# A deformable-convolution and attention kernel: batch 0's samples transposed by TensorE into two buffer sets, and three head groups that run chunks 4 and 5 apart

## The chip, the cores and the metric

The kernel runs on one core of one Trainium2 chip. The metric is the device time of one execution in microseconds; lower is better. Engines: TensorE (PE, with its weight load PEld), VectorE (DVE), ScalarE (ACT), GpSimd (POOL) and SyncE (SP, which here only issues DMAs).

## The reference

The input x is (4, 128, 64, 64) in float32: four batches, 128 channels, 64 x 64 positions. Cut to what matters:

```python
# layer 0: deformable 3x3 convolution on the group-normalized input
offset, mask = conv2d(gn(x), w_off), sigmoid(conv2d(gn(x), w_mask))   # 18 + 9 per position
samples = bilinear_sample(gn(x), position + tap + offset) * mask      # b, c, 9 taps, h, w
x = x + einsum("bckhw,ock->bohw", samples, w) + bias
# layer 1: tokens t = (b, 4096, 128)
z = layer_norm(t)
q = qz_ring(z.heads(16, 8) + rx)          # cosines and their products along the 8
attn = softmax(q @ q.T / sqrt(8)) @ q     # 16 heads, 4096 x 4096 scores each
x1 = layer_norm(z + attn @ w_comb.T + b_comb)
t = t + layer_norm(x1 + relu(zf(x1) @ w1.T + b1) @ w2.T + b2)
t = t + top2_of_8_experts(layer_norm(t))
```

Queries, keys and values are the same q, so the scores are symmetric: the exponentials of key chunk i against query chunk j, transposed, serve key chunk j against query chunk i.

## The kernel before

**Units of work.** A batch's 4096 positions are eight chunks of 512 (`NCH`, `CH`); the 16 heads are four groups of four (`NGRP`). One attention *step* is 128 keys of one group against one chunk of 512 queries: `scores` (L1261, TensorE into two PSUM tiles of tag `sc`, of which there are three), two exponentials of 128 x 1024 (L1270, ScalarE), `context` (L1281, TensorE, into the one accumulator `acc`; the row of ones in the values gives the softmax's denominator). A *run* is the steps of one group and one query chunk; `runs` lists them in order. `WHOLE` runs take all 32 steps at once. Batch 0's chunks become ready one after the other, so its first 26 runs (`opening`) and some after them take only the key chunks that are there: `FIRST` starts a sum, `MORE` and `LAST` go on with it; between them the sum lies in DRAM (`partd`, stored at L1126, loaded into `cu` at L1456). In the opening ScalarE takes the sum out of `acc` (L1491), and a sum loaded into `cu` is added by a product with the identity (L281 on `acc`); after it VectorE does both (L1493, L1495). `gifts` names the pairs of chunks where the exponentials are turned by VectorE (`turn`, L1140), stored (`etd`), fetched again (`fetch`, L1195) and used by a later run (`from_turned`, L1214) in place of its own steps.

**Making a chunk.** `prepare(b)` norms the batch, writes a table of corner values to DRAM, makes offsets and weights, and then `deform` goes through 96 units (chunk, three taps, 128 positions). A unit is three indirect DMAs of GpSimd (L625; `gather` keeps some units ahead), a weighting and two sums on VectorE (L645, L650, L651). The sampled values lie with positions on partitions, and the convolution needs channels there. For chunks 0 and 1 of batch 0 TensorE transposes a unit into the one PSUM bank `misc` (L662) and VectorE copies it into `sT_first` (L665). For all others VectorE transposes 32 x 32 blocks (L686) and the chunk goes out to `smd` in DRAM (L698) and comes back in the other order (L731, `sT`). `convolved` then does the convolution (`conv_ps`), adds x (`xr`, L758), and `features` makes q and its high and low parts (`hiT`, `loT`, L838, L839), copies the values into `fx` on GpSimd (L823), and stores the operands (`fqd` L827, `kTd` L846, `qTd` L847). `finish` does the work after the attention (projection, feed-forward, experts) for a chunk of which all four groups are done; up to two of them are under way.

**The order.** PE, DVE, SP and POOL run in the order in which the program issues (`tc.manual_schedule`). A planner, `Beside`, decides that order: it keeps a clock `now` that moves on `STEP` = 1.82 us a step, a due time of VectorE (`dve`), and a queue of generators (`prepare`, `finish`, `turned`) that yield what they want next (`need(pe, dve, lat, hold, after)`). At each step it lets in side work: TensorE pieces (`fills`, one a step or three, within `credit`) and VectorE pieces as long as VectorE is at most `backlog` behind. `hold=True` keeps the `misc` bank for one job, `hold=None` stands outside that lock. `later` issues a DMA or a GpSimd instruction at a due time. When no step can go on for want of a chunk, `force` lets side work in without a step.

The lines below are those that no other place of this text says.

```python
STEP = 1.82; RATE = 0.44; LATE = 0.50
NV = 3; NF2 = 11; NST = 3; NET = 2; NCU = 2
ps_s = ctx.enter_context(tc.tile_pool(name="ps_s", bufs=3, space=PSUM))
```

Of the kernel before, what the change touches and what calls it, by code (L numbers as in the profile page):

```python
# [22 lines left out]
P = 128  # L23
# [7 lines left out]
KK = 9  # L31
# [193 lines left out]
def kernel(  # L225
# [373 lines left out]
    def deform(b, tab, idx, wt, rest):  # L599
# [8 lines left out]
        def early(n):  # L608

            return b == 0 and n < 3 * 12  # L610
# [23 lines left out]
        for n, (ch, kg, j) in enumerate(units):  # L634
# [11 lines left out]
            if moved:  # L646
                yield need(pe=0.01, dve=ve(384))
                moved.pop()()
# [3 lines left out]
            if b == 0 and ch < 2:  # L652


                if n % 12 == 0:
                    while len(summed) < ch:
                        yield need(lat=0.5)
                    sT = big.tile([P, KK, CH], F32, tag="xs", name=f"sT_first{ch}")
                yield need(pe=tr(3), lat=FREE, hold=True)
                pt = misc(f"sT_ps{j}_{kg}")  # L660
# [3 lines left out]
                def move(sT=sT, kg=kg, i=j % 4, pt=pt):  # L664
                    nc.vector.tensor_copy(  # L665
                        sT[:, 3 * kg : 3 * kg + 3, P * i : P * (i + 1)],
                        pt[:, : 3 * P].rearrange("p (k c) -> p k c", c=P),
                    )
# [3 lines left out]
                if n % 12 == 11:  # L672
                    yield need(pe=0.01, dve=ve(384))
# [45 lines left out]
    def convolved(b, ch, sT=None):  # L719
# [4 lines left out]
        if not in_order:  # L724
            yield need(lat=2.5)

            sT = big.tile([P, KK, CH], F32, tag="xs", name=f"sT{b}_{ch}")

        def get(kg):
            for c in range(4):  # L730
                nc.sync.dma_start(  # L731
                    out=sT[32 * c : 32 * (c + 1), 3 * kg : 3 * kg + 3],
# [8 lines left out]
        for k in range(KK):  # L741
            if k == 2 and not in_order:
                get(2)
            for hf in range(2):
                last = k == KK - 1 and hf == 1
                yield need(pe=MM256, dve=ve(128, 4) if last else 0.0, lat=0.2 if last else FREE, hold=not last)
                if k == 0 and hf == 0:
# [3 lines left out]
                    sT[:, k, 256 * hf : 256 * (hf + 1)], k == 0 and hf == 0, last,  # L751
# [41 lines left out]
    def features(b, ch, x2, mean, rstd):  # L793
# [29 lines left out]
        beside.later(beside.dve, lambda: nc.gpsimd.tensor_copy(f4[:, :, :, :HD], q8))  # L823

        def put_values():
            for g in range(NGRP):
                nc.sync.dma_start(out=fqd[b % 2][ch][g], in_=fx[:, :, QG * g : QG * g + QL])  # L827

        beside.later(beside.dve + 2.0, put_values)
# [3 lines left out]
        yield need(pe=tr(4), dve=ve(512, 2))  # L833
# [5 lines left out]
        nc.vector.tensor_tensor(lo.bitcast(F32R), pt, hi, ALU.subtract)  # L839

        def put(part, fT):

            kd = kTd[b % 2][ch].rearrange("(h l r d) n -> l r h d n", l=2, r=2, d=HD)
            qd = qTd[b % 2][ch].rearrange("(h r l d) n -> l r h d n", l=2, r=2, d=HD)
            for rep in range(2):
                nc.sync.dma_start(out=kd[part, rep], in_=fT)  # L846
                nc.sync.dma_start(out=qd[part, rep], in_=fT)  # L847

        beside.later(beside.dve - ve(512), lambda: put(0, hi))
        beside.later(beside.dve, lambda: put(1, lo))  # L850
# [69 lines left out]
    def feed_forward(b, ch, x4, a4):  # L920

        z3 = [
# [42 lines left out]
        nc.vector.tensor_tensor(a4, a4, pf.rearrange("p (i c) -> p i c", c=C), ALU.add)  # L965
        m = work.tile([P, 4], F32, tag="ln_m", name=f"m2{b}_{ch}")
# [156 lines left out]
    def park_sums(g, sc, cu, when):  # L1123
# [6 lines left out]
        beside.later(when, put)  # L1130
# [96 lines left out]
    groups, done, active = {}, [], []  # L1227
# [67 lines left out]
    def gifts(b, g, sc):  # L1295
        first = (4 if g == NGRP - 1 else 3) if b == 0 else 0
        return [sc + 1] if first <= sc < NCH - 1 else []
# [35 lines left out]
    for sc in range(4):  # L1333
        add_run(0, NGRP - 1, sc, [4, 5], MORE)
    for g in (3, 0, 1, 2):
        for sc in range(4):
            add_run(0, g, sc, range(6 if g == 3 else 4, 8), LAST)
# [72 lines left out]
    with tc.manual_schedule(engines={PE, DVE, SP, POOL}):  # L1410
# [6 lines left out]
        while n < len(steps):  # L1417
# [20 lines left out]
            beside.fills = 3 if run < 12 else 1  # L1438
            if streaming:
                backlog = 1.5  # L1440
# [49 lines left out]
            if by_act:  # L1490
                nc.scalar.copy(cu, acc)  # L1491
            elif kind in (WHOLE, FIRST):
# [5 lines left out]
            else:  # L1498
                park_sums(g, sc, cu, beside.now + 3.0 if by_act else beside.dve)
# [75 lines left out]
```

## Time and profile before

| | |
|---|---|
| median of the runs | 7609.23 us (7607.39 to 7621.65, 3 runs) |
| profiled execution | 7579.71 us |
| its span, first to last instruction | 7576.5 us, 180754 instructions |
| busy: PE, DVE, ACT, POOL | 94%, 59%, 91%, 22% |
| mean granted TensorE clock | 0.968 |
| exponentials (L1270) | 7400, 6849.4 us busy |
| turned pieces (L1140) | 792 transposes, 396 stores and 396 fetches |

The profile shows one execution. Busy time of an engine is counted without its register, branch, semaphore and DMA-issuing instructions. A wait is put down to the event that came last before the engine went on. L12 is line 12 of the kernel; a line can be that of a helper, as L281 for every product in four column groups.

### The profile page before, as it was taken

The numbers are of one execution on the slowest core, as the hardware profiler recorded it, in microseconds if no ns is written. First come the engines' busy times: TensorE is split into PE (matmuls) and PEld (weight loads), VectorE is DVE, ScalarE is ACT, GpSimd is POOL, SyncE is SP. The second block draws the span as 40 slices with busy tenths as digits, with TensorE's granted clock in tenths as the row PEclk, the third lists the DMA queues.
The fourth block names the chain that finished last, engine by engine and source line by source line (L and its number), as shares of the span: only waits on it lengthen the run. The fifth ranks groups of instructions, "written<-read, shape, count | busy, mean of one in ns | idle before, by whom it ended". The sixth has DMA issues, their size and how long they took to land.

```text
span 7576.5 us, 180754 instructions
## 1 busy us (share of the span) xinstructions
PE 7113.9 (94%) x73848; PEld 2375.9 (31%) x73848; DVE 4465.9 (59%) x8950; ACT 6863.5 (91%) x7467; POOL 1653.2 (22%) x1326
## 2 busy tenths in 40 slices
PE   3688999899999999999999999999999999999997
PEld 2122222223333333333333323333333333333333
DVE  7755356667444877776544677775444554455434
ACT  0578999889999999999999998989999999999995
POOL 5544034443000433422000334431000000000000
PEclk6889999999999999999999999999999999999998
DMA  6777567978446878887655789897454466666661
GB/s 181 223 204 219 141 223 241 300 234 291 149 168 200 292 244 280 268 277 244 203 179 190 228 279 298 289 324 237 174 190 152 148 236 230 232 222 239 226 202 63
DMA packets 909788, 1689.51 MB, mean 223 GB/s; under 512 B 150754, under 2 KB 384124, under 8 KB 858268
## 3 DMA queue, kind: packets, MB, share of 16 engines
q1 hardware_dynamic: 809102, 1371.37, 54.9%
q0 software_dynamic: 92160, 302.06, 12.4%
q8 instruction: 579, 9.49, 0.5%
q10 hardware_dynamic: 7694, 4.52, 0.2%
q14 instruction: 253, 2.07, 0.1%
HBM read 1027.51 MB, written 650.14 MB: 221 GB/s over the span
## 4 chain that ended last, share of the span: by engine, by line
PE 80%; DMA 8%; DVE 4%; issue 2%; ACT 2%; SPq 1%; another core or an unknown queue 0%; POOL 0%; POOLq 0%; DVEq 0%; ACTq 0%
PE acc L1281 39%; PE sc L1261 24%; PE acc L1214 5%; PE e_ps L281 4%; PE conv_ps L281 3%; DMA et<-etd 2%; PE f_ps L281 2%; ACT e L1270 2%; DMA etd<-st 1%; DMA sT<-smd 1%; PE om_ps L533 1%; DMA smd<-tr 1%; DVE st L1140 1%; DVE v L645 1%; DMA cu<-part 1%
## 5 line engine op out<-in xcount | busy, mean ns | idle before, releaser
L1270 ACT ACTIVATE e<-sc 128x1024 f32<-128x1024 f32 x7400 | 6849.4, 1081 | 527.0 <-PE sc L1261 368.1
L1281 PE MATMUL acc<-e,qf 128*9 128x512 f32 (+1 forms) x29600 | 3938.3, 601 | 18.6 <-ACT cu L1491 7.5
L1261 PE MATMUL sc<-qT,kT 32*128 32x512 f32 x14800 | 2368.7, 499 | 153.3 <-ACT e L1270 84.8
L1261 PEld LDWEIGHTS sc<-qT,kT 32*128 32x128 f32 x14800 | 942.8, 183 | 3612.6 <-ACT e L1270 3130.4
L625 POOL DMA_INDIRECT v<-tab,idx x1152 | 1451.8, 1260 | 1579.3 <-DVE tr L686 956.2
L1140 DVE STREAM_TRANSPOSE st<-e 128x1024 f32<-128x1024 f32 x792 | 937.3, 1222 | 752.4 <-ACT e L1270 620.1
L1281 PEld LDWEIGHTS acc<-e,qf 128*9 128x9 f32 (+1 forms) x29600 | 682.4, 91 | 610.3 <-issue 346.8
L396 POOL TENSOR_TENSOR r<-ln_t,expo 128x4 f32<-128x4 f32 x96 | 112.2, 1169 | 3105.4 <-DVE ln_t L394 3057.0
L645 DVE TENSOR_TENSOR v<-v,wt 128x1536 f32<-128x1536 f32 x384 | 667.0, 1737 | 119.5 <-DMA v<-tab,idx 96.8
L1214 PE MATMUL acc<-et,qv 128*9 128x128 f32 x12672 | 506.4, 276 | 52.2 <-DMA et<-etd 44.6
L1065 DVE TENSOR_TENSOR eo<-e_ps,gt 128x512 f32<-128x512 f32 x256 | 175.2, 686 | 552.5 <-PE e_ps L281 547.5
L650 DVE TENSOR_TENSOR v<-v 128x768 f32<-128x768 f32 x384 | 367.2, 956 | 10.1
L281 PE MATMUL conv_ps<-sT,wconv_sb 128*32 128x256 f32 x4320 | 351.0, 399 | 15.7 <-DMA sT<-smd 11.6
L1214 PEld LDWEIGHTS acc<-et,qv 128*9 128x9 f32 x12672 | 270.0, 90 | 254.4 <-issue 212.6
L686 DVE STREAM_TRANSPOSE tr<-v 128x128 f32<-128x128 f32 x1080 | 249.4, 282 | 37.5 <-DMA etd<-st 28.7
L1493 DVE COPY cu<-acc 128x512 f32<-128x512 f32 x116 | 80.2, 692 | 306.3 <-PE acc L1281 260.8
L651 DVE TENSOR_TENSOR v<-v 128x384 f32<-128x384 f32 x384 | 215.7, 562 | 13.3
L396 POOL TENSOR_TENSOR rstd<-lt_t,expo 128x4 f32<-128x4 f32 x32 | 57.9, 1811 | 575.9 <-DVE lt_t L394 550.7
L281 PE MATMUL f_ps<-w_sb,h 128*32 128x128 f32 x4096 | 166.1, 282 | 0.1
L950 DVE TENSOR_SCALAR h<-h_ps,b_sb 128x512 f32<-128x512 f32 x128 | 94.9, 744 | 100.3 <-PE h_ps L948 89.9
L823 POOL COPY fx<-rn 128x512 f32<-128x512 f32 x32 | 26.8, 838 | 526.3 <-DVE rn L822 321.4
L965 DVE TENSOR_TENSOR a<-a,f_ps 128x512 f32<-128x512 f32 x32 | 21.9, 685 | 198.8 <-PE f_ps L281 198.8
(227 smaller groups left out, 3166.9 us busy)
## 6 DMA issues: line engine op xcount, KB each, us to landing
etd<-st SPq DMA_DIRECT2D x396, 1024.0 KB
et<-etd SPq DMA_DIRECT2D x396, 1024.0 KB
kT<-kTd SPq DMA_DIRECT2D x372, 256.0 KB
smd<-tr SPq DMA_DIRECT2D x360, 192.0 KB
sT<-smd SPq DMA_DIRECT2D x360, 192.0 KB
qT<-qTd SPq DMA_DIRECT2D x166, 256.0 KB
atd<-cu SPq DMA_DIRECT2D x128, 256.0 KB
qf<-fqd SPq DMA_DIRECT2D x372, 72.0 KB
```

What stands on the lines that cost most here:

```text
L281: nc.tensor.matmul(dst[c : c + 32], lhsT=lhsT[:, c : c + 32], rhs=rhs, start=start, stop=stop)
L625: nc.gpsimd.indirect_dma_start(out=v[:, k, :], out_offset=None, in_=tab, in_offset=bass.IndirectOffsetOnAxis(ap=idx[:, j, kk : kk + 1], ax ...
L645: nc.vector.tensor_tensor(v4, v4, w12[:, :, None].to_broadcast([P, 12, C]), ALU.mult)
L650: nc.vector.tensor_tensor(v[:, :, : 2 * C], v[:, :, : 2 * C], v[:, :, 2 * C :], ALU.add)
L651: nc.vector.tensor_tensor(v[:, :, :C], v[:, :, :C], v[:, :, C : 2 * C], ALU.add)
L686: nc.vector.transpose(out=tr9[:, k, :, j % 4, :], in_=v[:, k, :C].rearrange("p (c i) -> p c i", i=32),)
L1065: nc.vector.tensor_tensor(ws[hf], pe.rearrange("p (e c) -> p e c", c=C), gt[:, i, 4 * hf : 4 * (hf + 1), None].to_broadcast([P, 4, C]), AL ...
L1140: nc.vector.transpose(out=st[:, :, 2 * pr : 2 * pr + 2, :].rearrange("p o h (q j) -> p o (h q) j", j=32), in_=es[pr].rearrange("p h (q o i ...
L1214: nc.tensor.matmul(acc[32 * h : 32 * h + QW, P * kt : P * (kt + 1)], lhsT=qv[:, at : at + QW], rhs=e[:, :, h, 32 * t : 32 * (t + 1)], star ...
L1261: nc.tensor.matmul(ps[i // 2][:, i % 2, :], lhsT=kT[h : h + 32, P * (t % 4) : P * (t % 4 + 1)], rhs=qT[h : h + 32, :], start=True, stop=True,)
L1270: nc.scalar.activation(e, ps[pr], AF.Exp, scale=1.0 / math.sqrt(HD))
L1281: nc.tensor.matmul(acc[32 * h : 32 * h + width, :], lhsT=flat[:, first : first + width], rhs=es[h // 2][:, h % 2, :], start=(t == ts[0]), ...
```

## The change

- For all chunks of batch 0 the samples are transposed by TensorE, into a PSUM tile of tag `sc` and outside the lock of `misc`; the copy out is three copies of 128 columns. The target alternates between the tile `xs` (even chunks) and nine tiles of tag `f2` (odd chunks), and the next chunk's units wait for the convolution of the chunk before the last, not of the last. Gathers run four units ahead for the whole batch.
- In the opening the planner lets three TensorE pieces in per step for all 26 runs (before: 12), and VectorE may be 4.0 us behind (before: 1.5).
- For all batches: the copy into `fx` is VectorE's, after `loT`; operands are stored with one DMA for the values (before: four) and two for each of the high and low parts (before: four), with another order of the rows inside a head, the same for keys and queries.
- `feed_forward` waits while another one is under way (`heavy`).
- A partial sum of the opening is stored from ScalarE's queue straight after its copy.
- Groups 3, 2 and 1 take chunks 4 and 5 for query chunks 0 to 2 in runs of their own (before: group 3, query chunks 0 to 3), and the order of the groups is 3, 2, 1, 0 (before: 3, 0, 1, 2). `gifts` starts at chunk 3 for all groups of batch 0.

```diff
--- before.py
+++ after.py
@@ -607,7 +607,7 @@
 
         def early(n):
 
-            return b == 0 and n < 3 * 12
+            return b == 0
 
         def gather(last):
 
@@ -644,33 +644,41 @@
             yield need(dve=ve(1536), after=landed)
             nc.vector.tensor_tensor(v4, v4, w12[:, :, None].to_broadcast([P, 12, C]), ALU.mult)
             if moved:
-                yield need(pe=0.01, dve=ve(384))
+                yield need(dve=ve(128, 3))
                 moved.pop()()
             yield need(dve=ve(768) + ve(384))
             nc.vector.tensor_tensor(v[:, :, : 2 * C], v[:, :, : 2 * C], v[:, :, 2 * C :], ALU.add)
             nc.vector.tensor_tensor(v[:, :, :C], v[:, :, :C], v[:, :, C : 2 * C], ALU.add)
-            if b == 0 and ch < 2:
+            if b == 0:
 
 
                 if n % 12 == 0:
-                    while len(summed) < ch:
+                    while len(summed) < ch - 1:
                         yield need(lat=0.5)
-                    sT = big.tile([P, KK, CH], F32, tag="xs", name=f"sT_first{ch}")
-                yield need(pe=tr(3), lat=FREE, hold=True)
-                pt = misc(f"sT_ps{j}_{kg}")
+                    if ch % 2:
+                        sT = [
+                            work.tile([P, CH], F32, tag="f2", name=f"sT{ch}_{k}", bufs=NF2)
+                            for k in range(KK)
+                        ]
+                    else:
+                        sT = big.tile([P, KK, CH], F32, tag="xs", name=f"sT_first{ch}")
+                        sT = [sT[:, k] for k in range(KK)]
+                yield need(pe=tr(3), lat=FREE, hold=None)
+                pt = ps_s.tile([P, 2, 512], F32, tag="sc", name=f"sT_ps{j}_{kg}")[:, 0, :]
                 for k in range(3):
                     nc.tensor.transpose(pt[:, P * k : P * (k + 1)], v[:, k, :C], ident)
 
                 def move(sT=sT, kg=kg, i=j % 4, pt=pt):
-                    nc.vector.tensor_copy(
-                        sT[:, 3 * kg : 3 * kg + 3, P * i : P * (i + 1)],
-                        pt[:, : 3 * P].rearrange("p (k c) -> p k c", c=P),
-                    )
+                    for k in range(3):
+                        nc.vector.tensor_copy(
+                            sT[3 * kg + k][:, P * i : P * (i + 1)], pt[:, P * k : P * (k + 1)]
+                        )
 
                 moved.append(move)
                 beside.later(beside.now + 0.8, lambda n=n: gather(n))
                 if n % 12 == 11:
-                    yield need(pe=0.01, dve=ve(384))
+                    yield need(lat=0.6)
+                    yield need(dve=ve(128, 3))
                     moved.pop()()
                     featuring.append(True)
                     beside.add("prepare", convolved(b, ch, sT), 0.5, True)
@@ -724,12 +732,13 @@
         if not in_order:
             yield need(lat=2.5)
 
-            sT = big.tile([P, KK, CH], F32, tag="xs", name=f"sT{b}_{ch}")
+            sTs = big.tile([P, KK, CH], F32, tag="xs", name=f"sT{b}_{ch}")
+            sT = [sTs[:, k] for k in range(KK)]
 
         def get(kg):
             for c in range(4):
                 nc.sync.dma_start(
-                    out=sT[32 * c : 32 * (c + 1), 3 * kg : 3 * kg + 3],
+                    out=sTs[32 * c : 32 * (c + 1), 3 * kg : 3 * kg + 3],
                     in_=smd[ch % 2][:, 3 * kg : 3 * kg + 3, c].rearrange("i k o n -> i k (o n)"),
                 )
 
@@ -748,7 +757,7 @@
                     po = misc(f"conv_ps{b}_{ch}")
                 by_columns(
                     po[:, 256 * hf : 256 * (hf + 1)], wconv_sb[:, k, :],
-                    sT[:, k, 256 * hf : 256 * (hf + 1)], k == 0 and hf == 0, last,
+                    sT[k][:, 256 * hf : 256 * (hf + 1)], k == 0 and hf == 0, last,
                 )
         summed.append(True)
         for o in range(4):
@@ -820,34 +829,35 @@
         nc.vector.tensor_tensor(q8[:, :, :, 1], c8[:, :, :, 0], c8[:, :, :, 1], ALU.mult)
         for d in range(2, HD):
             nc.vector.tensor_tensor(q8[:, :, :, d], q8[:, :, :, d - 1], c8[:, :, :, d], ALU.mult)
-        beside.later(beside.dve, lambda: nc.gpsimd.tensor_copy(f4[:, :, :, :HD], q8))
-
-        def put_values():
-            for g in range(NGRP):
-                nc.sync.dma_start(out=fqd[b % 2][ch][g], in_=fx[:, :, QG * g : QG * g + QL])
-
-        beside.later(beside.dve + 2.0, put_values)
-
-
-
-        yield need(pe=tr(4), dve=ve(512, 2))
+
+
+
+        yield need(pe=tr(4), dve=ve(512, 3))
         pt = misc(f"fT_ps{b}_{ch}")
         for i in range(4):
             nc.tensor.transpose(pt[:, P * i : P * (i + 1)], n[:, P * i : P * (i + 1)], ident)
         hi, lo = temp("hiT"), temp("loT")
         nc.vector.tensor_copy(hi.bitcast(F32R), pt)
         nc.vector.tensor_tensor(lo.bitcast(F32R), pt, hi, ALU.subtract)
+        nc.vector.tensor_copy(f4[:, :, :, :HD], q8)
 
         def put(part, fT):
 
-            kd = kTd[b % 2][ch].rearrange("(h l r d) n -> l r h d n", l=2, r=2, d=HD)
-            qd = qTd[b % 2][ch].rearrange("(h r l d) n -> l r h d n", l=2, r=2, d=HD)
-            for rep in range(2):
-                nc.sync.dma_start(out=kd[part, rep], in_=fT)
-                nc.sync.dma_start(out=qd[part, rep], in_=fT)
-
-        beside.later(beside.dve - ve(512), lambda: put(0, hi))
-        beside.later(beside.dve, lambda: put(1, lo))
+            kd = kTd[b % 2][ch].rearrange("(p l r) n -> l p r n", l=2, r=2)
+            qd = qTd[b % 2][ch].rearrange("(p r l) n -> l p r n", l=2, r=2)
+            twice = fT[:, None, :].to_broadcast([P, 2, CH])
+            nc.sync.dma_start(out=kd[part], in_=twice)
+            nc.sync.dma_start(out=qd[part], in_=twice)
+
+        def put_values():
+            nc.sync.dma_start(
+                out=fqd[b % 2][ch].rearrange("g p t x -> p t g x"),
+                in_=fx.rearrange("p t (g x) -> p t g x", g=NGRP),
+            )
+
+        beside.later(beside.dve - 2.0 * ve(512), lambda: put(0, hi))
+        beside.later(beside.dve - ve(512), lambda: put(1, lo))
+        beside.later(beside.dve, put_values)
         prepared[b, ch] = beside.dve + 9.0
         featuring.pop(0)
 
@@ -919,6 +929,9 @@
 
     def feed_forward(b, ch, x4, a4):
 
+        while heavy:
+            yield need(lat=1.0)
+        heavy.append(True)
         z3 = [
             work.tile([P, 4, HD], F32, tag=f"zf{k}", name=f"zf{k}{b}_{ch}") for k in range(3)
         ]
@@ -963,6 +976,7 @@
                     f == 0, f == FFN // P - 1,
                 )
         nc.vector.tensor_tensor(a4, a4, pf.rearrange("p (i c) -> p i c", c=C), ALU.add)
+        heavy.pop()
         m = work.tile([P, 4], F32, tag="ln_m", name=f"m2{b}_{ch}")
         rs = work.tile([P, 4], F32, tag="ln_r", name=f"r2{b}_{ch}")
         yield from layer_norm_stats(a4, m, rs, "ln")
@@ -1120,14 +1134,14 @@
 
         beside.later(beside.dve, put)
 
-    def park_sums(g, sc, cu, when):
+    def park_sums(g, sc, cu):
 
         def put():
             nc.sync.dma_start(out=partd[g][sc], in_=cu)
             storing.discard((g, sc))
 
         storing.add((g, sc))
-        beside.later(when, put)
+        beside.later(beside.dve, put)
 
 
 
@@ -1224,7 +1238,7 @@
 
     landing = {}
     fetched = {}
-    groups, done, active = {}, [], []
+    groups, done, active, heavy = {}, [], [], []
 
     def finishing():
 
@@ -1293,8 +1307,7 @@
     gives, takes = set(), {}
 
     def gifts(b, g, sc):
-        first = (4 if g == NGRP - 1 else 3) if b == 0 else 0
-        return [sc + 1] if first <= sc < NCH - 1 else []
+        return [sc + 1] if (3 if b == 0 else 0) <= sc < NCH - 1 else []
 
 
     def add_run(b, g, sc, chunks, kind):
@@ -1330,11 +1343,12 @@
     opening = len(runs)
     for g in range(2, NGRP):
         extend(g, range(2), [2, 3], MORE)
-    for sc in range(4):
-        add_run(0, NGRP - 1, sc, [4, 5], MORE)
-    for g in (3, 0, 1, 2):
+    for g in (3, 2, 1):
+        for sc in range(3):
+            add_run(0, g, sc, [4, 5], MORE)
+    for g in (3, 2, 1, 0):
         for sc in range(4):
-            add_run(0, g, sc, range(6 if g == 3 else 4, 8), LAST)
+            add_run(0, g, sc, range(6 if g and sc < 3 else 4, 8), LAST)
         for sc in range(4, 8):
             add_run(0, g, sc, range(NCH), WHOLE)
 
@@ -1435,9 +1449,9 @@
                     gives.remove(steps[m])
                     turn(es[m - n], *steps[m])
 
-            beside.fills = 3 if run < 12 else 1
+            beside.fills = 3 if streaming else 1
             if streaming:
-                backlog = 1.5
+                backlog = 4.0
             else:
                 backlog = 0.4 if at >= len(ts) - 3 else 3.2
             if b + 1 < NB:
@@ -1489,14 +1503,15 @@
                 cu = work.tile([P, 512], F32, tag="cu", name=f"cu{run}", bufs=NCU)
             if by_act:
                 nc.scalar.copy(cu, acc)
+                nc.scalar.dma_start(out=partd[g][sc], in_=cu)
             elif kind in (WHOLE, FIRST):
                 nc.vector.tensor_copy(cu, acc)
             else:
                 nc.vector.tensor_tensor(cu, cu, acc, ALU.add)
             if kind in (WHOLE, LAST):
                 park_context(b, g, sc, cu)
-            else:
-                park_sums(g, sc, cu, beside.now + 3.0 if by_act else beside.dve)
+            elif not by_act:
+                park_sums(g, sc, cu)
         alone.append(True)
         beside.drain()
```

## The prediction

> **What bounds the kernel now.** I read the page first, then busy time by stage, then the waits and the chain of the first 900 us. From the page:
>
> ```profile
> PE 7113.9 (94%) x73848; PEld 2375.9 (31%) x73848; DVE 4465.9 (59%) x8950; ACT 6863.5 (91%) x7467; POOL 1653.2 (22%) x1326
> ACT  0578999889999999999999998989999999999995
> L1270 ACT ACTIVATE e<-sc 128x1024 f32<-128x1024 f32 x7400 | 6849.4, 1081 | 527.0 <-PE sc L1261 368.1
> ```
>
> One attention step (`steps[n]`, 128 keys against 512 queries of four heads) has two of these exponentials. 6849.4 us over 7400 is 0.926 us each (neighbours overlap, so less than the mean of one), 1.85 us a step for 3700 steps. ScalarE is the floor; the time can only move where ScalarE is idle, or by taking steps away. Its idle time is mostly early, so next the stages (columns: us, busy time and count of PE, PEld, DVE, ACT, POOL, then TensorE clock, DMA share, GB/s):
>
> ```profile
> 0.00:182.00 182.00, 61.42 (x559) 39.31 (x559) 127.42 (x211) 7.61 (x9) 98.32 (x84) 0.68 0.62 180
> 182.00:320.00 138.00, 78.37 (x685) 25.98 (x685) 102.16 (x188) 59.13 (x67) 84.67 (x63) 0.75 0.73 221
> 320.00:650.00 330.00, 277.14 (x2164) 76.80 (x2160) 200.52 (x365) 260.40 (x289) 160.67 (x123) 0.89 0.75 223
> 650.00:912.00 262.00, 246.21 (x1904) 69.66 (x1900) 130.96 (x266) 241.23 (x262) 60.96 (x47) 0.95 0.52 152
> 912.00:2246.00 1334.00, 1278.74 (x12190) 401.48 (x12186) 776.30 (x1424) 1237.13 (x1342) 387.89 (x311) 0.98 0.72 230
> 2246.00:5900.00 3654.00, 3548.07 (x38068) 1192.36 (x38068) 2311.73 (x4601) 3467.55 (x3764) 819.87 (x659) 0.99 0.72 238
> ```
>
> ScalarE idles 78.9 + 69.6 + 20.8 = 169 us between its first exponential (182) and 912, where batch 0's chunks are still being made; 97 us to 2246; 186 us to 5900. What it waits for in the first 900 us:
>
> ```profile
> ACT e L1270 <- PE sc L1261: 212.9, 41, 122.4
> PE sc L1261 <- DMA kT<-kTd: 46.9, 4, 22.0
> PEld acc L281 <- DMA cu<-part: 28.5, 5, 8.2
> ```
>
> Scores wait for keys of a chunk that is not yet there, context sums for a parked partial sum. The chain shows why the latter is late (start us, length):
>
> ```profile
> 261.38 5.98 DMA qf<-fqd
> 268.64 1.38 SPq L698
> 271.08 6.51 DMA sT<-smd
> 277.61 6.89 DMA cu<-part
> 284.54 1.93 PE acc L281 x8
> ```
>
> On SP's queue the partial sum stands behind the samples' trip through DRAM (L698 out, L731 back). By the timeline, batch 0's chunks have their operands issued to DRAM at 162, 254, 356, 471, 580, 692, 793 and 875: 82 to 115 us apart. The attention has done 16 steps at 221, 64 at 390, 104 at 477, 160 at 641, 256 at 826; it cannot pass 16, 64, 104 and 256 steps without chunks 1, 2, 3 and 4/5. It waits for chunk 1 (45.6 us at 222) and chunk 3 (14.0 at 478). The other 110 us are small: partial sums 28.5, `conv_ps` behind samples 9.4, the key load behind batch 1's border DMAs at 890 10.8, the rest in gaps under 5 us.
>
> **The change, part by part.** *Samples by TensorE, two buffer sets.* One unit (three taps of 128 positions) on VectorE now:
>
> ```profile
> 207.83 1.75 DVE L645 TENSOR_TENSOR v<-v,wt 128x1536 f32<-128x1536 f32 x1
> 209.62 0.96 DVE L650 TENSOR_TENSOR v<-v 128x768 f32<-128x768 f32 x1
> 210.61 0.56 DVE L651 TENSOR_TENSOR v<-v 128x384 f32<-128x384 f32 x1
> 211.20 0.70 DVE L686 STREAM_TRANSPOSE tr<-v 128x128 f32<-128x128 f32 x3
> ```
>
> That is 4.0 us. In chunks 2 to 7 (72 units) the last row gives way to three 128x128 copies out of PSUM. The trace has 128x384 at 0.551 and 128x512 at 0.69, so 0.27 each and 0.82 a unit: 4.1 us. Features take 19 us of VectorE per chunk (the sum of L758 to L839 in the timeline) and 0.6 more for the copy into `fx` (GpSimd's median 0.612; no VectorE row of this shape, a 128x512 tensor_tensor takes 0.69). A chunk is 12 x 4.1 + 19.6 = 69 us of VectorE and 36 x (1.31 + 0.30) = 58 us of gathers, against 105 us between chunks now. What held it there goes: the DRAM trip, two units gathered ahead instead of four, `len(summed) < ch`, and the 1.5 us that VectorE might be behind in the opening. At 75 us a chunk, chunk 2 is there near 330, chunk 3 near 405 and chunk 7 near 700, each before the attention asks. The GpSimd copy, for which gathers stood in line (98.5 us idle before seven of them), is gone as well.
>
> TensorE gets 216 transposes; three of them start 0.109 us apart at 190.7, so 24 us over some 500 us. A step needs about 1.29 us of TensorE (scores 0.43, context 0.86 by start times at 812), so 1.85 - 1.29 a step hides them. [...]
>
> *What is new on TensorE's queue.* The transposes wait in order for the sums of a VectorE that may now be 4 us behind, and all scores and context products queue behind them; and they sit in one of the three `sc` buffers until the copies, one multiply later, some 3 of every 4 us. No row shows this with attention at full rate. The nearest are three units at 182 to 192, where ScalarE had gaps of 3.89, 1.72 and 1.58 us: 2.4 a unit. The other end is 0, if the slack takes it. I take 0.5 (36 us for 72 units): those three stood behind VectorE waiting 2.07 and 0.86 us for gathers, with ScalarE one step ahead; later four units are gathered ahead and TensorE is late itself, so VectorE is mostly done.
>
> *Partial sums stored from ScalarE's queue*, 26 of them, each behind its copy, with the next exponential behind it. From SP the issue takes 0.33 us; with the copy's 0.585 waited out, 0.91. So 9 to 24 us; I take 0.6 each, 16 us. It frees SP, which waited 113.8 us for these copies. [...]
>
> *Three groups with [4, 5] apart.* Chunks 6 and 7 are asked for at step 328 instead of 288, so the 10.8 us at 890 are covered. Nine such runs replace four: five more accumulator hand-overs at 29.3/72 = 0.4 us, +2. One more chunk is turned instead of recomputed: four steps fewer, -7.4.
>
> *Batches 1 to 3.* Twelve operand DMAs a chunk become five, and SP no longer stands before `fqd` for GpSimd:
>
> ```profile
> SPq L827 <- POOL fx L823: 171.7, 26, 14.2
> SPq L1195 <- PE acc L1214: 590.7, 159, 9.5
> ```
>
> Behind it are the turned tiles (L1195), for which TensorE waited 44.6 + 32.9 us. At best half of that, 40, comes back; at worst VectorE's 32 x 0.6 = 20 is added; `heavy` only spaces the feed-forward parts, with nothing late behind it in the trace. I take -12.
>
> **The sum.** ScalarE's idle time from 182 to 912: 169 becomes 35 (chunk 1, a little earlier by SP's shorter queue) + 5 (partial sums) + 20 (small gaps) + 16 + 36 = 112, so -57. With -7, +2 and -12: -74. The profiled execution took 7579.7 (span 7576.5 and 3.2 around it), which gives 7506; the median of the runs is 29.5 higher, so 7609 - 74 = 7535.
>
> **The rivals.** *TensorE's order costs the gain (slower).* At 2.4 us for each of 72 units, 173 instead of 36: 63 us slower, 7672. It decides from 1.5 us a unit. For it: the three gaps at 182. Against: TensorE waiting that long means VectorE is the limit, and 69 us a chunk leave it idle a third of the time at today's rate. *All cover holds.* No cost on the queue (-36), 9 for the stores (-7), 40 back in the later batches (-28): 7464. For it: nothing but ScalarE bounds after 5900, so each gap closed is kept. *Nothing arrives.* The 110 us of small gaps are the planner's, not the chunks', and stay at 75 rather than 25: 7585 to 7610. [...]
>
> **How the numbers follow.** Forecast (7500 to 7585) 0.58, all cover holds 0.17, nothing arrives 0.11, slower 0.14. About 0.2%, 15 us, is what a measurement of this kernel can tell from no change: faster is the first two and a third of the third, 0.79; same 0.07; slower 0.14. The range leaves out the ends of both outer cases: 7455 to 7610.
>
> **What would show it.** Right: 7392 exponentials; operands of chunk 7 stored near 700; 160 steps done near 555 instead of 641; ScalarE idle some 110 us in its first 730; TensorE's clock above 0.9 from 320 on; no `smd` before batch 1. Wrong: `sT_ps` waits on VectorE of over 1.5 us a unit, chunks still 100 us apart, or idle time after 912 that grows by what the opening gave.

## The result and the profile after

The change made the kernel slower: 7680.7 us (median of 4 runs, 7674.25 to 7697.35) against 7608.3 for the kernel before (4 runs beside them), a ratio of 1.0097, 95% interval 1.0075 to 1.0119, 72 us. The profiled execution took 7697.35 (span 7695.5), 17 above the median, where that of before lay 29 below its own; so the two traces stand 118 us apart and show some 45 more than the change is worth.

The page of the kernel after, the same three lines as before:

```profile
PE 7167.8 (93%) x74144; PEld 2403.9 (31%) x74144; DVE 4478.0 (58%) x9043; ACT 6865.9 (89%) x7459; POOL 1600.2 (21%) x1294
ACT  0678998898999988988999988889999999999995
L1284 ACT ACTIVATE e<-sc 128x1024 f32<-128x1024 f32 x7392 | 6851.0, 1076 | 649.6 <-PE sc L1275 464.8
```

The floor held: 7392 exponentials, 6851.0 us, 0.927 us each. What grew is ScalarE's idle time before an exponential, 649.6 us against 527.0, and the eights in its row stand in the middle of the program as well as at its beginning. Busy time by stage of the kernel after (us, busy time and count of PE, PEld, DVE, ACT, POOL, then TensorE clock, DMA share, GB/s):

```profile
182.00:320.00 138.00, 95.46 (x734) 32.77 (x734) 95.92 (x197) 61.87 (x68) 77.68 (x63) 0.78 0.58 182
320.00:650.00 330.00, 287.74 (x2238) 88.84 (x2230) 208.68 (x404) 255.82 (x281) 145.69 (x117) 0.92 0.57 173
650.00:912.00 262.00, 242.67 (x1915) 70.22 (x1917) 120.24 (x237) 239.81 (x258) 56.09 (x48) 0.96 0.43 132
912.00:2246.00 1334.00, 1261.43 (x12190) 398.59 (x12183) 790.44 (x1441) 1225.53 (x1327) 382.83 (x304) 0.98 0.74 239
2246.00:5900.00 3654.00, 3475.83 (x36912) 1163.54 (x36908) 2249.22 (x4455) 3368.01 (x3655) 797.76 (x640) 0.98 0.71 234
```

ScalarE's idle time: 172.5 us from 182 to 912 (169.2 before, 112 forecast), 108.5 to 2246 (96.9 before), and 286.0 from 2246 to 5900, where it was 186.5. So the opening gained nothing, and the loss is almost all in batches 1 and 2, which the change hardly seems to touch. Waits of the kernel after from 182 to 912 (engine, tile, line, what ended the wait; us in total, times, longest):

```profile
ACT e L1284 <- PE sc L1275: 110.0, 82, 33.0
ACT cu L1505 <- PE acc L281: 26.8, 7, 14.8
PE acc L281 <- DMA cu<-part: 10.5, 1, 10.5
PE sT_ps L669 <- DVE v L651: 14.3, 7, 4.3
POOL v L625 <- PE sT_ps L669: 266.5, 30, 32.9
```

The wait for keys (`kT<-kTd`) is gone, as is most of that for partial sums. TensorE's transposes wait 14.3 us in all for VectorE; gathers wait 266.5 us for TensorE's transposes, which free their `v` tiles. In batches 1 and 2, 2246 to 5900 us, the kernel before had

```profile
ACT e L1270 <- PE sc L1261: 96.3, 89, 8.1
PE acc L1214 <- DMA et<-etd: 20.7, 8, 6.7
PE conv_ps L281 <- DMA sT<-smd: 4.1, 2, 3.8
```

and the kernel after

```profile
ACT e L1284 <- PE sc L1275: 169.8, 113, 14.9
PE acc L1228 <- DMA et<-etd: 52.7, 15, 9.6
PE conv_ps L281 <- DMA sT<-smd: 20.8, 4, 13.7
```

TensorE, in order, waits longer and more often for the turned tiles that it uses instead of recomputing exponentials, and for samples that come back from DRAM (chunks of batches 1 to 3 still take that way); ScalarE waits for the scores queued behind them. These two waits grew by 49 us; the rest of the 99 is spread over other waits.

### The profile page after: what moved, and what is told of

Same layout as the page of the kernel before. It is cut to its first block, busy times and chain, and to the rows that moved or that the text cites. A ratio compares the mean times of both kernels' runs of the same rounds, so it can differ in the third digit from the quotient of the medians.

```text
span 7695.5 us, 180911 instructions
## 1 busy us (share of the span) xinstructions
PE 7167.8 (93%) x74144; PEld 2403.9 (31%) x74144; DVE 4478.0 (58%) x9043; ACT 6865.9 (89%) x7459; POOL 1600.2 (21%) x1294
## 4 chain that ended last, share of the span: by engine, by line
PE 81%; DMA 7%; DVE 4%; ACT 3%; issue 3%; SPq 1%; POOL 1%; another core or an unknown queue 1%; ACTq 0%; POOLq 0%; DVEq 0%
PE acc L1295 39%; PE sc L1275 24%; PE acc L1228 5%; PE conv_ps L281 4%; PE e_ps L281 3%; ACT e L1284 3%; DMA et<-etd 2%; PE f_ps L281 2%; DMA sT<-smd 1%; POOL v L625 1%; PE om_ps L533 1%; DVE v L645 1%; SPq L730 1%; PE ao_ps L281 1%
## 5 line engine op out<-in xcount | busy, mean ns | idle before, releaser
L1284 ACT ACTIVATE e<-sc 128x1024 f32<-128x1024 f32 x7392 | 6851.0, 1076 | 649.6 <-PE sc L1275 464.8
L625 POOL DMA_INDIRECT v<-tab,idx x1152 | 1436.1, 1247 | 2212.1 <-DVE tr L694 1340.4
L281 PE MATMUL conv_ps<-sT,wconv_sb 128*32 128x256 f32 x4032 | 328.9, 401 | 47.9 <-DMA sT<-smd 39.8
L694 DVE STREAM_TRANSPOSE tr<-v 128x128 f32<-128x128 f32 x864 | 199.0, 281 | 31.6 <-DMA etd<-st 25.0
L669 PE MATMUL sT_ps<-ident,v 128*128 128x128 f32 x288 | 64.0, 341 | 117.4 <-DVE v L651 76.0
L281 PEld LDWEIGHTS conv_ps<-sT,wconv_sb 128*32 128x32 f32 x4032 | 85.6, 109 | 175.8 <-issue 154.1
```

The source lines that it names most:

```text
L281: nc.tensor.matmul(dst[c : c + 32], lhsT=lhsT[:, c : c + 32], rhs=rhs, start=start, stop=stop)
L625: nc.gpsimd.indirect_dma_start(out=v[:, k, :], out_offset=None, in_=tab, in_offset=bass.IndirectOffsetOnAxis(ap=idx[:, j, kk : kk + 1], ax ...
L694: nc.vector.transpose(out=tr9[:, k, :, j % 4, :], in_=v[:, k, :C].rearrange("p (c i) -> p c i", i=32),)
L1284: nc.scalar.activation(e, ps[pr], AF.Exp, scale=1.0 / math.sqrt(HD))
```

## The experiments

Theories. *Order*: TensorE's queue and the `sc` tile cost what the earlier chunks gain. *Plan*: the opening gains, and other parts of the change (guard, store block, runs) shift side work of the later batches to where TensorE waits. Kernels were measured in sets, each beside runs of the kernel before. Its medians lay between 7461 and 7614 us from set to set, so what is compared across sets is the ratio to its runs in the same set. That a ratio carries over from one set to another was not measured.

**Parts of the change, alone or taken away.** In the change, the guard is on from `feed_forward`'s first line to its sum:

```diff
     def feed_forward(b, ch, x4, a4):
+        while heavy:
+            yield need(lat=1.0)
+        heavy.append(True)
...
         nc.vector.tensor_tensor(a4, a4, pf.rearrange("p (i c) -> p i c", c=C), ALU.add)
+        heavy.pop()
```

b_heavy: the kernel before with only these lines.

> The kernel before with one part of the change alone: feed_forward waits while another one is under way. In the changed kernel ScalarE idles 286 us from 2246 to 5900 instead of 186. Theory 'heavy' (feed-forward parts in single file push the other side work together): this run loses 60 to 100 us in batches 1 and 2, 7670 to 7710. Theory 'stores' (the merged operand stores and the values' copy on VectorE do it) and theory 'opening' (all of it comes from batch 0): 7600 to 7620, batches 1 and 2 as before.

1.0039 [1.0025, 1.0054]. The edit that the forecast put at nothing costs 30 us alone.

b_heavy_stores: the same, and the change's whole store block (copy into `fx` on VectorE after `loT`, five DMAs, values last).

> The kernel before with heavy, the merged operand stores and the copy into fx on VectorE, nothing of batch 0's part. Theory 'stores': 60 to 100 us slower than the run with heavy alone, at 7670 to 7710, in batches 1 and 2, with TensorE waiting more for turned tiles. Theory 'heavy': the same as the run with heavy alone. Theory 'opening': as before, 7600 to 7620.

1.0061 [1.0044, 1.0078]: the block adds 0.22% (the two intervals overlap a little) and gives nothing back. By the traces it adds this at the very end: behind the last exponential 107 us are left where b_heavy has 90, while batches 1 and 2 lose as much in both (249 and 248 us, counted as in the table below).

a_old_stores: the change with the store block of before (copy by GpSimd, twelve DMAs).

> The changed kernel with the old operand stores (twelve DMAs a chunk, fx copied by GpSimd). Theory 'stores': batches 1 and 2 get 60 to 100 us back, 7590 to 7620. Theories 'heavy' and 'opening': 7670 to 7700.

1.0048 [1.0032, 1.0065]: half of the loss goes with the block.

a_misc: the change with the samples in a `misc` bank under its lock, so that `sc` is left to the scores.

```diff
-                yield need(pe=tr(3), lat=FREE, hold=None)
-                pt = ps_s.tile([P, 2, 512], F32, tag="sc", name=f"sT_ps{j}_{kg}")[:, 0, :]
+                yield need(pe=tr(3), lat=FREE, hold=True)
+                pt = misc(f"sT_ps{j}_{kg}")
```

> The changed kernel with the samples' transposes in the one misc bank again, under its lock, instead of one of the three sc tiles. ScalarE idled 150 us from 182 to 650 in the changed kernel, in some thirty small gaps. Theory 'sc tile' (scores have two tiles instead of three for most of the time): 30 to 50 us of these go, 7635 to 7655, if the lock does not slow the chunks. Theory 'order' (TensorE waits in order for VectorE's sums, in whatever bank): no change in the small gaps, 7670 to 7700.

1.0073 [1.0056, 1.0089]. Step 160 comes 36 us sooner than in the change, but chunk 7's operands are stored at 927 us instead of 876, ScalarE then idles 24.6 us in one piece (in 12.7 of them TensorE waits for keys), and the opening's gain is given back by 2246. So the shared tile costs something early, and sharing the lock costs as much later.

a_batch0_only: the change without the guard and with the old store block.

> The changed kernel without heavy and with the old operand stores: what is left of the change touches batch 0 alone (TensorE samples, two buffer sets, planner's limits, three groups, sums from ScalarE's queue). heavy alone cost 30 us on the kernel before, the stores 20 to 32. Theory 'sum of parts': batch 0's part is worth nothing, 7600 to 7630, ScalarE idle some 150 us in the opening's 160 steps as before, batches 1 and 2 as before. Theory 'the parts need each other' (batch 0's part shifts all that follows): 7640 to 7660.

1.0006 [0.9995, 1.0017]. Without guard and block the loss is gone, and what is left of the change gains nothing.

a_old_runs: the change with the old store block and the old runs (group 3 alone, four query chunks, `gifts` as before).

> The changed kernel with the old operand stores, and with the old order of runs (one group has chunks 4 and 5 apart, groups 3, 0, 1, 2). In the changed kernel chunks 6 and 7 were stored at 777 and 877, and it reached step 288 at 911. Theory 'cover' (the longer list hides the late chunks): without it a wait of 10 to 30 us at step 288, 7655 to 7680. Theory 'no use' (chunks are there in time either way): 7640 to 7655.

1.0008 [0.9998, 1.0019]. Against a_old_stores (of another set), guard or runs each give 0.4% when taken away.

a_sums_by_sp: the change with the old store block and partial sums stored from SP's queue.

> The changed kernel with the old operand stores, and with the opening's partial sums stored from SP's queue as before. Theory 'ScalarE pays for the issue': 10 to 24 us faster than the run with the old stores alone (7648), so 7625 to 7640, all of it in the first 160 steps. Theory 'free' (ScalarE idles there anyway): no difference within 10 us, or slower if sums come late again.

1.0033 [1.0020, 1.0045], overlapping a_old_stores.

b_merged_dma: the kernel before with one DMA for the values and two for each part, at the old places.

```diff
-            for rep in range(2):
-                nc.sync.dma_start(out=kd[part, rep], in_=fT)
-                nc.sync.dma_start(out=qd[part, rep], in_=fT)
+            twice = fT[:, None, :].to_broadcast([P, 2, CH])
+            nc.sync.dma_start(out=kd[part], in_=twice)
+            nc.sync.dma_start(out=qd[part], in_=twice)
```

> The kernel before with the operand DMAs merged and nothing else: the same plan, fx still copied by GpSimd, the values' DMA at its old place. Theory 'burst' (the same bytes posted in five DMAs hold up what is behind them): 15 to 30 us slower, 7630 to 7645, with TensorE waiting more for turned tiles. Theory 'VectorE' (the copy of fx on VectorE and its place in the plan is what costs): 7605 to 7620.

0.9979 [0.9969, 0.9988]: fewer DMAs gain by themselves.

b_fx_vector: the kernel before with the copy into `fx` on VectorE, straight after the products, the plan's figures unchanged.

```diff
-        beside.later(beside.dve, lambda: nc.gpsimd.tensor_copy(f4[:, :, :, :HD], q8))
+        nc.vector.tensor_copy(f4[:, :, :, :HD], q8)
```

> The kernel before with the copy into fx done by VectorE right after the products, everything else and the plan's estimates as before. heavy plus all of the stores was 0.22% slower than heavy alone, the merged DMAs alone were 0.21% faster than before, so some 0.4% (33 us) lies in the copy and in what the plan makes of it. Theory 'copy' (0.47 us of VectorE each, 32 times, and what waits behind it): 15 us or more slower, ratio 1.002 to 1.005. Theory 'plan' (the copy is free, the 0.7 us that the plan sets aside for it shifts all that follows): ratio 0.998 to 1.001.

0.9974 [0.9965, 0.9983]: VectorE's copy gains too, which neither theory had. Both contents of the store block gain alone, so its cost does not lie in their work.

b_heavy_runs: the kernel before with the guard and the new runs.

> The kernel before with heavy and the new runs (three groups have chunks 4 and 5 apart, order 3, 2, 1, 0), chunks made as before. heavy alone was at 1.0039. The changed kernel with the old stores went from 1.0048 to 1.0008 when it got the old runs back. Theory 'runs cost' (five more hand-overs and twice as many reloads, or the order of groups): 1.006 to 1.009. Theory 'runs cost only together with early chunks': 1.002 to 1.005.

1.0042 [1.0029, 1.0056], as the guard alone: the runs moved nothing there.

**The opening without the rest.** m_mix keeps the samples by TensorE, the two buffer sets, the larger limits and the merged DMAs; it has the old runs, GpSimd's copy, sums by SP, and the guard only from the transposes of `z` on:

```diff
 def feed_forward(b, ch, x4, a4):
-        while heavy:
-            yield need(lat=1.0)
-        heavy.append(True)
...
+        while heavy:
+            yield need(lat=1.0)
+        heavy.append(True)
         yield need(pe=tr(4), dve=ve(512), lat=0.2)
         pz = misc(f"z_ps{b}_{ch}")
```

> A mix: batch 0's samples by TensorE with two buffer sets and the planner's new limits, merged DMAs, but fx copied by GpSimd, the old runs, sums stored by SP, and the guard on feed_forward only from its transposes to its last product. By the sum of parts (merged -0.21%, sums by SP -0.15%, old runs -0.4%, heavy mostly gone -0.3%, against 1.0048): 0.993 to 0.997. If the parts' gains do not add: 0.998 to 1.002.

0.9932 [0.9918, 0.9945], 7404.5 us against 7461.4: faster than the kernel before and, by the ratios, than the change. No run parts the narrower guard from the rest of it. m_early_copy is m_mix with each copy out of `sc` before the next unit's multiply, not after it:

```diff
-                moved.append(move)
                 beside.later(beside.now + 0.8, lambda n=n: gather(n))
+                yield need(dve=ve(128, 3))
+                move()
```

> The mix, with a unit's samples copied out of the sc tile before the next unit's multiply instead of after it: the tile was held 204 us in all, up to 15 us at a time while VectorE made features. Theory 'sc tile' (scores short of a tile make the opening's small gaps): 15 to 40 us of ScalarE's idle time from 182 to 650 go, and the run is 0.2 to 0.5% faster than the mix. Theory 'order' (TensorE's program stands still for VectorE's sums and VectorE for TensorE's transposes): no gain, or slower, since VectorE now waits for each transpose.

0.9960 [0.9947, 0.9974], slower than m_mix. Giving the `sc` tile back one multiply sooner gained nothing, but in VectorE's order each copy now stands straight behind its transposes, and the order theory expected no gain from this too: the run doesn't part the two.

**One part back at a time into m_mix.** f_wide has the guard at the change's place, f_stores the change's store block, f_runs its runs, f_sums its partial sums (stored from ScalarE's queue), f_limits the kernel before's limits (`backlog = 1.5`, three pieces for 12 runs); f_fx has one edit more, b_fx_vector's.

> m_mix with one thing of the change back: the feed-forward waits for the other one from its first line (the change's place), not from its transposes. If the guard's place is a cause of its own, it costs here what it costs alone in the kernel before (0.39%) and in the change (0.42%): a ratio of 0.996 to 0.998 instead of 0.993, with ScalarE's idle time in 2246 to 5900 us up by 15 us or more. If only its being there matters and not its place, 0.992 to 0.994. If it costs only together with the change's other parts, 0.993 as well, so that theory is told apart by the other three kernels of this set.

> m_mix with the change's whole store block back: the copy into fx by VectorE after the low part, 0.7 us more of VectorE set aside for it, the values' DMA last. If the block costs by itself (it was 0.49% in the change, 0.22% in the kernel before with the guard): 0.995 to 0.998. If it costs only by pushing a plan that the guard and the new runs have made tight: 0.991 to 0.993, since the copy by VectorE was worth 0.26% alone in the kernel before.

> m_mix with the change's runs back (three groups with chunks 4 and 5 apart, three query chunks, order 3, 2, 1, 0). Four steps fewer and five more hand-overs give -5 us, 0.9925, if only the sum of steps counts, as in the kernel before with the guard, where the runs moved nothing. If the runs cost where chunks come early (0.40% in the change), 0.996 to 0.998: then the opening's stage 182 to 650 is unchanged, and it is the next 96 steps and batch 1 that lose.

> m_mix with one edit that is not the change's: the copy into fx is issued on VectorE where the plan has GpSimd's, with the plan's figures as they are. If its gain in the kernel before (0.26%) came from GpSimd's copy standing in line with the gathers, which this kernel still has: 0.990 to 0.992, the fastest of all. If it came from one schedule by chance, 0.993 or a little above.

> m_mix with the opening's partial sums stored from ScalarE's queue again, as the change does. By the forecast's price (26 stores at 0.6 us) ScalarE loses 16 us before step 160 and TensorE gets its partial sums earlier: +0 to +16 us, 0.993 to 0.995. In the change, taking it away gave 0.15% (11 us). If it is what made the change's opening (loss of 171 us before step 160) worse than m_mix's (123): a loss of 140 or more here and 0.996.

> m_mix with the opening's limits of the kernel before: VectorE planned up to 1.5 us behind (not 4.0), three pieces a step in the first 12 runs only. If letting more in is what lets the chunks come early: chunk 7's operands stored 40 us or more later, step 160 later by 20 us or more, 0.996 or above. If more side work let in is what stretches the steps to 2.0 to 2.4 us while chunks are made: 0.990 to 0.992. If the one gives back what the other costs: 0.993.

The third column of the table is the price against m_mix (the quotient of the two ratios), the last is ScalarE's loss by stage: the time that the trace takes for these steps less 1.851 us a step, in batch 0's first 160 steps / its next 96 / its rest / batch 1 / batch 2. Losses are of one trace each and compare only between rows whose kernel before had like medians: 7608 us (before, after), 7461 to 7466 (b_fx_vector to f_fx) and 7588 (f_sums, f_limits).

| kernel | ratio, 95% interval | against m_mix | loss by stage, us |
|---|---|---|---|
| before (first trace) | 1 | | 163 / 8 / 109 / 82 / 108 |
| after (first trace) | 1.0097 [1.0075, 1.0119] | | 171 / 21 / 113 / 141 / 150 |
| b_fx_vector | 0.9974 [0.9965, 0.9983] | | 143 / -1 / 83 / 42 / 76 |
| m_mix | 0.9932 [0.9918, 0.9945] | | 123 / 12 / 84 / 22 / 57 |
| f_wide | 0.9976 [0.9967, 0.9984] | +0.44% | 121 / 12 / 83 / 65 / 60 |
| f_stores | 0.9993 [0.9983, 1.0003] | +0.61% | 125 / 20 / 85 / 51 / 77 |
| f_runs | 0.9988 [0.9980, 0.9997] | +0.56% | 120 / 12 / 97 / 43 / 80 |
| f_fx | 0.9883 [0.9866, 0.9899] | -0.49% | 121 / 13 / 70 / 22 / 55 |
| f_sums | 0.9933 [0.9920, 0.9945] | +0.01% | 134 / 12 / 106 / 66 / 96 |
| f_limits | 1.0016 [1.0006, 1.0026] | +0.85% | 116 / 13 / 145 / 87 / 101 |

Guard, store block and runs each cost by themselves, and hardly in the opening: 46, 48 and 44 us (before rounding) of what they lose against m_mix fall in batches 1 and 2. Put together with the sums, 0.9932 x 1.0044 x 1.0061 x 1.0056 x 1.0001 is 1.0094; the change measured 1.0097. The factors' own intervals leave that product open by about 0.45% to either side, so a match this close is luck. But the parts are enough for the change's loss, and m_mix, which has the order theory's queue and shared tile, is faster than the kernel before: the order theory is not needed.

f_fx and f_stores differ in no work of VectorE: both copy `fx` there, with the same merged DMAs. They lie 1.1% apart. Only where the plan puts the copy and the values' store, and the 0.7 us more that it sets aside for VectorE, tell them apart. f_fx is the fastest of all: 7381.8 us against 7465.6, 84 us below the kernel before.

Where such a loss arises is seen in f_stores: the chain of waits behind one of its stops, where ScalarE idled 10.1 us at 2996.6 (start us, length, what):

```profile
2973.12 2.37 DVE st L1154 x2
...
2980.41 0.20 SPq L1163
2980.61 0.05 issue
2980.66 0.02 SPq L1209
2980.67 0.03 issue
2980.70 22.41 DMA et<-etd
3003.12 0.04 issue
3003.16 1.04 PE acc L1228 x16
```

VectorE turns two tiles, SP stores them (L1163) and then issues the load of an older one (L1209), which lands 22.41 us later; the planner had set 16 (`beside.now + 16.0`). In those 22 us the DMA engines were full (busy tenths of 2981 to 3003 in 40 slices, f_stores):

```profile
DMA  9999999899999999999999999999999999999999
```

Twelve gathers, four loads of samples and two stores of turned tiles were issued in them. One stop of f_wide, at 4976.8, has the same shape (there too that row is all nines but for one eight):

```profile
4960.35 0.02 SPq L1210
4960.40 21.50 DMA et<-etd
4981.95 1.04 PE acc L1229 x16
```

TensorE's waits for turned tiles over batches 1 and 2, in m_mix, f_fx, f_wide, f_stores and f_runs, in this order:

```profile
PE acc L1229 <- DMA et<-etd: 22.1, 11, 6.0
PE acc L1229 <- DMA et<-etd: 20.3, 10, 6.8
PE acc L1229 <- DMA et<-etd: 38.7, 14, 7.3
PE acc L1228 <- DMA et<-etd: 57.7, 15, 8.7
PE acc L1229 <- DMA et<-etd: 49.9, 13, 9.5
```

The three slower kernels wait 17, 36 and 28 us more than m_mix, of the 46, 48 and 44 us that they lose there. Elsewhere such waits don't tell the loss: b_fx_vector has 35.7 us of them and loses 118, f_sums 5.5 us and loses 162. That the late landing comes from these bursts is read from the traces; no run removed the bursts alone.

f_limits is the one edit whose code acts in the opening alone. Its first 160 steps are the quickest of all, but its chunk 7 is stored at 883 us, not at 827 as in f_sums, and between 600 and 912 it has

```profile
ACT e L1285 <- PE sc L1276: 52.3, 30, 37.3
PE sc L1276 <- DMA kT<-kTd: 11.8, 1, 11.8
```

where f_sums, on the same chip, has

```profile
ACT e L1285 <- PE sc L1276: 9.4, 17, 2.2
```

One stop of 37.3 us, for a chunk that is not there: this is what the larger limits save in batch 0, and more than the 18 us between the two kernels before step 160 (f_sums has the sums on ScalarE's queue as well). It is not all that parts them. Of the 78 us between their traces 26 fall in batches 1 and 2, and 30 behind the last exponential, which the table leaves out: there f_limits still has 490 TensorE products to do and takes 110 us, f_sums 393 and 80 us.

## Why the prediction was wrong

The sign was wrong, and the time lies where the forecast had its slower rival (7672), but not by that rival's mechanism.

*The floor and the count of steps held*: 7392 exponentials at 0.927 us. No `smd` trip before batch 1 and TensorE's clock above 0.9 from 320 on (0.92, 0.96) held too.

*Chunks 75 us apart: failed.* Chunks 1 to 7 are stored (low parts of the queries) at 250, 347, 443, 546, 648, 775 and 876 us: 104 apart, as before. The 75 was VectorE's work, 69, and little else. The work was right: 208.7 us busy in 320 to 650, 65 for every 102 us. What was left out stands in the same window of the change:

```profile
DVE xr L767 <- PE conv_ps L281: 49.1, 3, 17.9
DVE hiT L840 <- PE fT_ps L838: 26.1, 4, 7.7
DVE sT_first L673 <- PE sT_ps L669: 20.4, 7, 11.1
DVE sT L673 <- PE sT_ps L669: 14.6, 13, 3.7
```

That is 110 us of VectorE waiting for TensorE, 34 a chunk, for convolution, transposes of features and samples, each queued behind attention. Working time and these waits make 99 of the 102. The trace that the forecast was made from had the largest of them in the same window:

```profile
DVE xr L758 <- PE conv_ps L281: 44.1, 2, 23.9
```

The forecast's sum has no term for it. This chain, which goes from engine to engine and back, had the work and the waits as its period (99 of 102 us), not the busier engine's work alone (65). Without the other parts (m_mix) chunk 7 is stored at 815, 96 us a chunk: better, still far from 75.

*Idle 112 us from 182 to 912: failed, 172.5.* The wait for chunk 1 was right (33.0, forecast 35); one copy of ScalarE waited 14.8 us behind a late partial sum, where 5 were forecast for all. The rest, small gaps and stores and order together, is 124.7 where the forecast had 20 + 16 + 36 = 72. Of this, order is not the cause that the rival named: TensorE waited 14.3 us for VectorE's sums, 0.2 a unit where the rival needed 1.5. In m_mix, with the same queue, step 160 is done at 601 us (641 before, 555 forecast), but these two traces are of sets 2% apart. In m_mix's own set b_fx_vector, which makes its chunks as before but for the copy into `fx`, has done step 160 at 620 and step 256 at 797 (m_mix 790), and over batch 0 it loses 225 us against 219. Against it the opening gains about 20 us by step 160 and gives most of it back by the end of batch 0; m_mix leads by what it loses less in batches 1 and 2, 79 us against 118. The 555 does not follow from the forecast's own sum either: 160 steps of 1.85 from 182 on with its 112 us of idle time end at 590, and 555 leaves the 36 us on TensorE's queue out. What took the opening's gain back in the change is not settled: each part put back alone leaves 120 to 125 us of loss before step 160, as m_mix has, and the sums 134 in a slower set. In the change, taking the store block away brings that loss from 171 to about 145 (a_old_stores, before at 7614), one trace each.

*Sums by ScalarE, 16 us: nothing.* In the change's trace the instruction behind such a copy starts 0.48 us after the copy's start (median of 26), as in the kernel before, with the store's issue of 0.33 us beside it. f_sums gives 0.9933 against 0.9932 in another set, so the 23 us for earlier partial sums (28.5 to 5) didn't come either.

*Five runs, +2 less four steps, -7: failed.* f_runs is 0.56% (42 us) behind m_mix instead of 5 ahead, although on the kernel before, with the guard, the runs were free (1.0042 against 1.0039).

*Batches 1 to 3, -12: the term that made the sign.* ScalarE's idle time from 2246 to 5900 grew by about 100 in the traces, of which up to 45 is the two profiled executions' distance from their medians. Its parts: merged DMAs gain 0.21% and VectorE's copy 0.26%, more than was counted; but `heavy`, "with nothing late behind it", costs 0.39% alone and 0.44% in m_mix, and the block as the change places it 0.61%. The forecast priced each edit by the work that it adds; that is the step that failed. Of 7608 us, m_mix is worth -52, the guard's place +33, block +46, runs +43 and sums +1. What each edit did was to move feed-forward and operand work of later chunks against the attention. That transfers then meet the turned tiles' loads, for which TensorE waits in order, is seen at single stops and in part of the loss; the rest has no cause shown.

*The transposes.* The 288 transposes (L669) took 64.0 us of TensorE, 0.222 each, twice the 0.109 between starts that the forecast used; one by itself lasted 0.341 in the mean, since neighbours overlap. That did not make the result, since m_mix has the same transposes and gains (0.9932). What the transposes do to the clock no run shows: from 320 to 650 it was 0.92 with them and 0.89 without.

Left open: why these three edits, and not others, land in an unlucky plan, and which part of m_mix makes its gain in batches 1 and 2. f_runs being free in one plan and 0.56% in another, and f_fx and f_stores 1.1% apart with the same work, say that the price belongs to the schedule as much as to the edit.

## What to carry to other kernels

In a kernel whose side work is placed by a planner, an edit's own work is the smaller part of its price: put it alone into the kernel, and look at stages far from where it acts. Price a chain that runs through two engines by the sum of work and waits of a period, from the waits of the engine that is only half busy. When a change bundles several edits, put them back one at a time into the best mixture: here a mixture and four edits put back multiplied out to the whole within the noise, and the mixture with one edit more turned 1% slower into 1.2% faster. Count the time behind the last stage too: two kernels here lost 17 and 30 us there, which no table by stage showed.

## What the hardware showed

- The same kernel's median went from 7461 us in one set to 7614 in another, 2%; a figure from another set would have hidden every effect here. Two sets on chips of the same number, 2, had 7584 and 7461, so the chip is not shown to be the reason.
- Two loads of a turned tile took 22.41 (f_stores) and 21.50 us (f_wide) to land while the DMA engines were full (39 of 40 slices at nine tenths or more), where the planner counts on 16.
- Fewer, larger DMAs of the same bytes (five instead of twelve a chunk) gained 0.21% [0.12, 0.31] in a kernel whose bound is ScalarE.
- The 26 DMAs issued from ScalarE's queue did not hold up ScalarE in the median: the next instruction started 0.48 us after the start of the copy before it, with the 0.33 us of issue (the change) or without (the kernel before).
